# Four GNN layers on one core: the last layer by seven products of half matrices, logits spread on TensorE, statistics stored in two parts

## The chip, the cores and the metric

The kernel runs on one core of one Trainium2 chip. The metric is the device time of one execution in microseconds (us); the median of 12 runs of the kernel before is 2025.46 us (2020.86 to 2029.03). The engines of the core are TensorE (PE in the profile; PEld is its weight load), VectorE (DVE), ScalarE (ACT), GpSimd (POOL) and SyncE (SP). Each takes its instructions in the order in which they were compiled. SP, ACT and POOL also issue DMAs, each on its own queue; SPq, ACTq and POOLq in the profile are these issues.

## The reference

Input are x, 2708 nodes by 256 features, and adj, a sparse 2708 x 2708 matrix with a full diagonal, all float32. Four layers follow each other, each as `x = layernorm(x + layer(x, adj))`:

- layer 0: `adj @ (x * W)`
- layer 1: attention with four heads of 64 features over the mask `adj > 0`, then a layer norm
- layer 2: two supports and two GRU cells. With A = adj without its diagonal: `edge_output = gru(A @ h, h)`, and for each of three heads `hW = h @ W`, a logit e per node from the sums of hW over its neighbours, `att = softmax` over the columns with A > 0 of e, and `att * A @ hW`. The mean over the heads goes through the second GRU cell, `node_output`. The result is `diag * (edge_output + node_output)`
- layer 3: `h = adj @ (x @ neigh_W.T) / (rowsum(adj) + 1)` and `z = [x, h] @ lin_W.T`

The logits e depend on the column alone, so that the softmax needs for each row and head a maximum and a denominator: the row statistics.

## The kernel before, in words

The nodes lie in 22 tiles of 128 rows (NT; the last has 20). Six spans of 4 or 3 tiles order the work of layer 1 and the edge half of layer 2. For the node half the matrix is cut in two halves of 1354 nodes (NH, 11 tiles: MH), and the columns of both halves in three units of 512, 512 and 330 (`units`).

Layer 2, edge half: `edge_logits` (L484) makes the logits of each span, writes them to DRAM (`e_d`, L507, six stores on POOL's queue), and three DMAs on ACT's queue (L788) read them back as `e_b`, the same 2708 numbers on all 128 partitions, per head. `row_stats` then makes the statistics of each row tile: a custom VectorE operation (L816) for the maximum and an exponential with a sum on ACT (L821), 66 of each. `edge_sums` (L241) multiplies A by h for a span, `edge` runs the first GRU cell on it (`gru_t`, L724) and stores the result (`edge_d`, L830). `xt_d` and `edge_d` are DRAM tensors with x and the edge output transposed. At the end `store_rows` turns the statistics of all tiles (`store_stats`, L757-773: transposes on PE, a copy to `sr` on ACT, stores on POOL's queue). The node half reads them back on SP (`load_stats`, L882).

Layer 2, node half (L1062-1126): for each unit, each head and each of 11 pairs of row tiles (c and c + 11) a step loads the blocks of adj (`load_blocks`, L898 on SP, 9 or 7 DMAs of two 128 x 128 blocks each; a block on the diagonal is masked on POOL, L901), builds four quarter blocks of attention (ACT Relu L1076, Exp L1079, DVE L1080), forms three sums of quarters on DVE (L1085-1088), and runs seven products instead of eight (L1099) into seven PSUM banks, with sums of the quarters of x that `x_sums` makes on POOL, four subtractions of 128 x 128 for each c. The seven accumulators are `m1`, `m26`, `m75`, `m43`. After 11 steps they are added up to `y`.

What follows from a unit is cut into tasks, run in the one PSUM bank left, after the third and the sixth product of a step (`between`): `project` (L928) multiplies by the head's weights, `node` loads `xt2` and `et` (L234 on SP), runs the second GRU cell (`cell`, L945, L959) and the row ends: `node_rows` (L983), `rows_turned` (L997), `rows_end` (L1006). The last makes the input of layer 3, `h3` (x @ neigh_W.T and lin_W already multiplied in), and the part of the output that doesn't need adj, stored as `y3_d` (L1013). The tasks of the last unit, four of `project` and 37 of `node`, run after the last product, with eight PSUM banks (L1127-1130).

Layer 3 (`layer3`, L1133-1146) loads for each row tile a strip of adj, 128 rows of 11 KB in one DMA on SP (L180), and multiplies it by the 22 tiles of h3, each in two passes of 256 columns (`strip_matmul`, L201). The last operations of a tile: load `o` from y3_d (L1139 on SP), one DVE operation (L1142), layer norm (L148-159, with a power on POOL, L153), the store of the output on POOL's queue (L1146).

The instructions of an engine are put in order at compile time by a list scheduler. A DMA issued on SP or ACT waits for the DMA eight before it, since eight semaphores are shared in turn.

Of the kernel before, what the change touches and what calls it, by code (L numbers as in the profile page):

```python
# [27 lines left out]
def kernel(  # L28
# [100 lines left out]
    e_d = dram.tile([K, N], F32, name="e_d")  # L129
# [3 lines left out]
    xt_d = dram.tile([P, FC, N], F32, name="xt_d")  # L133
    edge_d = dram.tile([P, FC, N], F32, name="edge_d")
# [96 lines left out]
    def load_columns(pool, d, lo, w, tag, bufs=1):  # L231

        dst = pool.tile([P, FC, W], F32, tag=tag, name=tag, bufs=bufs)
        nc.sync.dma_start(dst[:, :, :w], d[:, :, lo : lo + w])  # L234
        return dst
# [3 lines left out]
    edges = []  # L239

# [60 lines left out]
    if True:  # L301
# [14 lines left out]
        if True:  # L316
# [145 lines left out]
            if True:  # L462
# [21 lines left out]
                def edge_logits(pool, rows):  # L484

                    evs = rows.tile([P, len(banks), W], F32, tag="supt", name="evs", bufs=2)
                    for b, w, acc in zip(banks, bw, pu):
                        full = len(b) * CT
                        parts = pool.tile([P, W], F32, tag="parts", name="parts")
                        nc.scalar.copy(parts[:full, :w], acc[:full, :w])  # L490
                        pe = ps_t.tile([P, 4, P], F32, tag="tr", name="pe").rearrange("p i q -> p (i q)")
                        nc.tensor.matmul(
                            pe[: K * TILES, :w], add_parts[:full].rearrange("p k j -> p (k j)"), parts[:full, :w],
                            start=True, stop=True,
                        )
                        ev = evs[: K * TILES, b.start // TILES]
                        nc.scalar.copy(ev[:, :w], pe[: K * TILES, :w])
                        nc.vector.scalar_tensor_tensor(ev[:, :w], ev[:, :w], ALPHA, ev[:, :w], ALU.mult, ALU.max)
                        pc = ps_t.tile([P, 4, P], F32, tag="tr", name="pc")
                        for i in range(w // P):  # L500
                            nc.tensor.transpose(
                                pc[:, i, : K * TILES], ev[:, i * P : (i + 1) * P], ident[: K * TILES, : K * TILES]
                            )
                        for j, g in enumerate(b):
                            lo, hi = spans[g]
                            gw = width(lo, hi)
                            nc.gpsimd.dma_start(e_d[:, lo * P : lo * P + gw], ev[j : K * TILES : TILES, :gw])  # L507
                            nc.vector.tensor_scalar(
                                e_neg[:, lo:hi, :],
                                pc[:, : hi - lo, : K * TILES].rearrange("p i (k j) -> p i k j", j=TILES)[:, :, :, j],  # L510
                                -1.0, None, ALU.mult,
                            )
# [37 lines left out]
                def layer1_logits(pool, t, m, fill, split, gap):  # L550
# [3 lines left out]
                    nc.gpsimd.dma_start(xt_d[:, :, t * P : t * P + n], xt[:, :, :n])  # L554
# [202 lines left out]
    def store_stats(ps, pool, lo, hi):  # L757

        at, w = lo * P, width(lo, hi)
        pt = ps.tile([P, 4, P], F32, tag="tr", name="pst")  # L760
# [5 lines left out]
        sr = pool.tile([2 * K, W], F32, tag="sr", name="sr")  # L766
# [11 lines left out]
    with pool("e_work") as ework:  # L778
        with (
# [7 lines left out]
            for k in range(K):  # L787
                nc.scalar.dma_start(e_b[:, k], bcast(e_d[k], N))  # L788
# [8 lines left out]
            def row_stats(i):  # L797
# [15 lines left out]
                for k in range(K):  # L813
                    z = rows.tile([P, N], F32, tag="z", name="z", bufs=3)
# [11 lines left out]
            def edge(g, supt, xt):  # L826
                at, w = spans[g][0] * P, width(*spans[g])
                yt = ework.tile([P, FC, W], F32, tag="yt", name="yt")
                gru_t(ps_g, ework, yt, supt, xt, w, wih, whh, b_edge)
                nc.scalar.dma_start(edge_d[:, :, at : at + w], yt[:, :, :w])  # L830

            stored = 0

            def store_rows(done):

                nonlocal stored
                while stored < done:
                    n = 1
                    while n < 4 and stored + n < done and order[stored + n] == order[stored] + n:
                        n += 1  # L840
                    store_stats(ps_e, rows, order[stored], order[stored] + n)
                    stored += n

            for g, (lo, hi) in enumerate(spans):
                for i in range(lo, hi):
                    row_stats(i)
                last = g + 1 == len(spans)
                if last:
                    store_rows(lo)
# [7 lines left out]
            store_rows(NT)  # L857
# [5 lines left out]
    with (  # L863
# [20 lines left out]

        def load_blocks(u, c):
# [21 lines left out]
        ts = []  # L907

        def x_sums(c):
            tt = nleft.tile([P, 4, P], F32, name=f"xq{c}")  # L910
            b11, b12 = xs[c][:, :P], xs[c][:, P:]
            b21, b22 = xs[c + MH][:, :P], xs[c + MH][:, P:]
            nc.gpsimd.tensor_tensor(tt[:, 0], b12, b11, ALU.subtract)
            nc.gpsimd.tensor_tensor(tt[:, 1], b22, tt[:, 0], ALU.subtract)
            nc.gpsimd.tensor_tensor(tt[:, 2], b12, b22, ALU.subtract)
            nc.gpsimd.tensor_tensor(tt[:, 3], b21, tt[:, 1], ALU.subtract)
            ts.append(tt)
# [63 lines left out]
        shared = {}  # L981
# [32 lines left out]

        def node(u, est):
# [3 lines left out]
            for h in range(2):  # L1019
                lo = h * NH + a  # L1020
                xt, et = nxt or [load_columns(nleft, d, lo, w, tag) for d, tag in ((xt_d, "xt2"), (edge_d, "et"))]
# [3 lines left out]
                tiles, at = [], 0  # L1025
                for t, c0, c1 in pieces(lo, w):
                    src = yt[:, :, at : at + c1 - c0]
                    at += c1 - c0
                    if c1 - c0 < sz(t):
                        first = t not in shared  # L1030
                        if first:
                            shared[t] = nleft.tile([P, FC, P], F32, name=f"yt{t}")
                        nc.gpsimd.tensor_copy(shared[t][:, :, c0:c1], src)
                        if first:
                            continue
                        src = shared[t]
                    tiles.append((t, src))
                got, turned = [], []
                for i in range(len(tiles) + 2):
# [9 lines left out]
                    if i == 1 and h == 0:  # L1049
                        nxt = [load_columns(nleft, d, NH + a, w, tag) for d, tag in ((xt_d, "xt2"), (edge_d, "et"))]  # L1050
# [11 lines left out]
        for u, (_, w) in enumerate(units):  # L1062
            est = [nleft.tile([P, FC, W], F32, tag="est", name="est", bufs=3) for h in range(2)]
            for k in range(K):
                m1 = ps_a.tile([P, W], F32, tag="m1", name="m1")
                m26, m75, m43 = (ps_a.tile([P, 2, W], F32, tag=nm, name=nm) for nm in ("m26", "m75", "m43"))
                for c in range(MH):
                    if u == 0 and k == 0:
                        x_sums(c)
                    blk = load_blocks(u, c)  # L1070
                    pa = []
                    for i in range(2):
# [8 lines left out]
                        pa += [p[:, 0, :w], p[:, 1, :w]]  # L1081
                    a11, a21, a12, a22 = pa
                    s = nright.tile([P, 3, W], F32, tag="s", name="s", bufs=2)
                    s1, s2, s4 = (s[:, i, :w] for i in range(3))
                    nc.vector.tensor_tensor(s1, a21, a22, ALU.add)  # L1085
                    nc.vector.tensor_tensor(a21, a21, a11, ALU.subtract)  # L1086
                    nc.vector.tensor_tensor(s2, s1, a11, ALU.subtract)
                    nc.vector.tensor_tensor(s4, a12, s2, ALU.subtract)
                    tt = ts[c]
                    for i, (dst, lt, rt) in enumerate((  # L1090
                        (m1, xs[c][:, :P], a11),
                        (m26[:, 0], xs[c + MH][:, :P], a12),
                        (m75[:, 0], tt[:, 2], a21),
                        (m75[:, 1], tt[:, 0], s1),
                        (m26[:, 1], tt[:, 1], s2),
                        (m43[:, 0], tt[:, 3], a22),
                        (m43[:, 1], xs[c + MH][:, P:], s4),
                    )):
                        nc.tensor.matmul(dst[:, :w], lt, rt, start=(c == 0), stop=(c == MH - 1))  # L1099
                        if i in (2, 5):  # L1100
                            between()
                    if u == 0 and k == 0 and c == 2:
                        node_w = load_weights()
                    if c == MH - 3:
# [5 lines left out]
                t1 = nleft.tile([P, W], F32, tag="m1s", name="m1s")  # L1110
                nc.scalar.copy(t1[:, :w], m1[:, :w])

                y = nleft.tile([P, FC, 2, W], F32, tag="yk", name="yk")
                yq = y.rearrange("p f h w -> p (f h) w")[:, :, :w]
                nc.vector.tensor_tensor(
                    yq[:, 0::3], t1[:, None, :w].to_broadcast([P, 2, w]), m26[:, :, :w], ALU.add
                )
                nc.vector.tensor_tensor(
                    yq[:, 1:3], yq[:, 3:4].to_broadcast([P, 2, w]), m75[:, :, :w], ALU.add
                )  # L1120
                nc.vector.tensor_tensor(yq[:, 3], yq[:, 1], m75[:, 1, :w], ALU.add)
                nc.vector.tensor_tensor(yq[:, 1:3], yq[:, 1:3], m43[:, :, :w], ALU.add)
# [3 lines left out]
            later.append(node(u, est))  # L1126
        ps_stack.close()  # L1127
# [19 lines left out]

    layer3()

# [246 lines left out]
```

## Time and profile before

| | |
|---|---|
| median of 12 runs | 2025.46 us |
| the profiled execution | 2024.36 us |
| its span | 2022.6 us |
| mean granted clock of TensorE | 0.981 |
| busy: PE, DVE, ACT, POOL | 95%, 67%, 43%, 16% |
| passes of layer 3 on PE (968) | 209.25 us |
| loads of adj for layer 3 on SP | 22 of up to 1408 KB |
| loads of blocks for the node half on SP (L898) | 825 issues, 0.54 to 1.76 us each, median 0.61 |
| landing after issue: 54 and 74 KB blocks, o, out | 2.5, 2.0, 3.5 us |

The span is what the engines' instructions cover; the execution's own time is 1.8 us longer. A line of a chain or a timeline gives the start in us from the span's start, the length in us, the engine, the line of the kernel and the number of instructions in a row. A line of waits gives the engine and line that waited, after the arrow what ended the wait, then the sum in us, how many times, and the longest. A line of windows gives a stretch, and for each engine its busy time and the number of its instructions.

### The profile page before, as it was taken

What the parts mean: (1) busy time and instruction counts of PE and PEld (TensorE: products, weight loads), DVE (VectorE), ACT (ScalarE), POOL (GpSimd) and SP (SyncE); (2) the same over time, 40 slices, a digit from 0 to 9 for tenths busy, and PEclk for the clock granted to TensorE, in tenths of its full rate; (3) what the DMA queues carried; (4) which work ended last, traced back from release to release, by engine and by line L of the source; (5) the groups of instructions that cost most, each with busy time, mean ns of one, the idle gap of its engine ahead of it and who ended that gap; (6) DMA issues with size and microseconds to landing.
All of it is one profiled execution on the core that took longest, in us unless ns stands there. A gap on an engine that the chain in (4) does not pass through costs nothing. (4 is left out here: it accounts for less than half of the span.)

```text
span 2022.6 us, 21703 instructions
## 1 busy us (share of the span) xinstructions
PE 1916.6 (95%) x7454; PEld 1032.2 (51%) x7454; DVE 1358.0 (67%) x2123; ACT 871.9 (43%) x995; POOL 329.8 (16%) x532
## 2 busy tenths in 40 slices
PE   8999999999999899999679999999999999889997
PEld 7888722222333334455333444444445656458886
DVE  4334388898897489999478789685876868431111
ACT  0100145446413167777656766565565656110000
POOL 0212110015324220111221001010100111011111
PEclk9999999999999999999889999999999999889999
DMA  8344333432104786664357766454553535214543
GB/s 283 130 149 164 107 132 116 143 132 96 34 9 111 269 262 213 201 210 139 109 157 200 193 175 175 123 161 111 158 151 99 151 94 133 81 43 175 188 178 107
DMA packets 334115, 296.49 MB, mean 147 GB/s; under 512 B 85836, under 2 KB 311030, under 8 KB 322946
## 3 DMA queue, kind: packets, MB, share of 16 engines
q1 hardware_dynamic: 318474, 245.28, 39.9%
q0 software_dynamic: 8512, 41.14, 5.6%
q10 hardware_dynamic: 7008, 8.58, 1.2%
q8 instruction: 61, 1.00, 0.2%
q14 instruction: 60, 0.49, 0.1%
HBM read 283.16 MB, written 11.76 MB: 146 GB/s over the span
## 5 line engine op out<-in xcount | busy, mean ns | idle before, releaser
L201 PE MATMUL acc<-turn,strip 128*128 128x256 f32 (+1 forms) x1804 | 396.4, 379 | 0.0
L201 PEld LDWEIGHTS acc<-turn,strip 128*128 128x128 f32 (+1 forms) x1804 | 331.7, 186 | 53.4 <-issue 1.3
L654 DVE SCALAR_TENSOR_TENSOR p<-fall_b,rise,mask 128x1024 f32<-128x1024 f32 (+1 forms) x264 | 298.9, 1154 | 37.4 <-PE den L645 19.8
L1076 ACT ACTIVATE p<-st,e_neg 128x1024 f32<-128x1024 f32 (+1 forms) x198 | 206.8, 1046 | 222.9 <-PE m L1099 218.4
L636 PE MATMUL acc<-p,h 128*64 128x512 f32 (+2 forms) x1056 | 228.0, 560 | 4.7 <-DVE p L654 2.7
L1080 DVE TENSOR_TENSOR p<-p,blk 128x1024 f32<-128x1024 f32 (+1 forms) x132 | 147.4, 1121 | 101.9 <-ACT p L1079 57.4
L816 DVE CUSTOM_DVE_ANT_0 z<-e_b,none 128x2708 f32<-128x2708 f32 (+1 forms) x66 | 196.5, 2983 | 15.2 <-DMA e_b<-e_d 15.2
L821 ACT ACTIVATE z<-z,st 128x2708 f32<-128x2708 f32 (+1 forms) x66 | 168.5, 2554 | 65.0 <-DVE st L816 63.5
L1099 PE MATMUL m<-p,x 128*128 128x512 f32 (+1 forms) x396 | 170.1, 548 | 25.7 <-DVE p L1080 22.2
L1079 ACT ACTIVATE p<-p 128x1024 f32<-128x1024 f32 (+1 forms) x198 | 188.9, 956 | 5.6
L1099 PE MATMUL m<-p,xq 128*128 128x512 f32 (+1 forms) x396 | 182.8, 544 | 1.6 <-DVE p L1086 0.9
L254 PE MATMUL s<-blk,x 128*128 128x512 f32 (+2 forms) x416 | 165.4, 552 | 4.7 <-DMA blk<-in_adj_t_dram 3.5
L1099 PE MATMUL m<-s,xq 128*128 128x512 f32 (+1 forms) x396 | 168.2, 542 | 0.0
L153 POOL TENSOR_TENSOR bn_rs<-bn_rs,neg_half 128x1 f32<-128x1 f32 (+1 forms) x110 | 75.5, 688 | 425.6 <-DVE bn_rs L152 425.5
L636 PEld LDWEIGHTS acc<-p,h 128*64 128x64 f32 x1056 | 65.2, 137 | 150.5 <-issue 119.1
L645 PE MATMUL den<-p,h 128*32 128x512 f32 (+2 forms) x1056 | 125.0, 554 | 2.3 <-DVE p L654 1.9
L1099 PEld LDWEIGHTS m<-p,x 128*128 128x128 f32 x396 | 74.8, 191 | 101.5 <-issue 62.2
L254 PEld LDWEIGHTS s<-blk,x 128*128 128x128 f32 x416 | 78.7, 192 | 82.1 <-issue 67.4
L1142 DVE SCALAR_TENSOR_TENSOR o<-acc,rdeg,o 128x256 f32<-128x256 f32 (+1 forms) x22 | 10.6, 483 | 155.8 <-PE acc L201 155.8
L1099 PEld LDWEIGHTS m<-p,xq 128*128 128x128 f32 x396 | 74.6, 190 | 78.1 <-issue 56.6
L1099 PEld LDWEIGHTS m<-s,xq 128*128 128x128 f32 x396 | 74.2, 190 | 74.5 <-issue 64.8
L167 ACT COPY xt<-tr 128x256 f32<-128x256 f32 (+1 forms) x44 | 16.0, 364 | 209.2 <-PE tr L165 203.4
(200 smaller groups left out, 2366.5 us busy)
## 6 DMA issues: line engine op xcount, KB each, us to landing
strip<-in_adj_t_dram SPq DMA_DIRECT2D x41, 1408.0 KB, 6.0
blk<-in_adj_t_dram SPq DMA_DIRECT2D x411, 128.0 KB, 2.7
turn<-in_adj_dram SPq DMA_DIRECT2D x22, 1354.0 KB, 5.8
turn<-in_adj_t_dram SPq DMA_DIRECT2D x204, 128.0 KB, 2.7
blk<-in_adj_t_dram SPq DMA_DIRECT2D x84, 256.0 KB, 5.7
arow<-in_adj_dram POOLq DMA_DIRECT2D x10, 1354.0 KB, 6.8
turn<-in_adj_dram POOLq DMA_DIRECT2D x10, 1354.0 KB, 6.7
st<-st SPq DMA_DIRECT2D x12, 512.0 KB, 4.5
```

The lines of the kernel that those rows point to most:

```text
L153: nc.gpsimd.tensor_tensor(rstd[:n], rstd[:n], neg_half[:n], ALU.pow)
L201: nc.tensor.matmul(acc, s[:, c, :n], rhs(c), start=(c == 0), stop=(c == NT - 1))
L254: nc.tensor.matmul(acc[f][:, :w], xs[c][:, f * P : (f + 1) * P], s[:, c - c0, :w], start=(c == 0), stop=(c == NT - 1),)
L636: nc.tensor.matmul(acc[s][i * HD : (i + 1) * HD, :ws], hs[c][:, 2 * q + i, :HD], ps[i][:, p0 : p0 + ws], **flags,)
L645: nc.tensor.matmul(den[j : j + CT, :ws], hs[c][:, 2 * q + i, HD + 1 - CT :], ps[i][:, p0 : p0 + ws], **flags,)
L654: nc.vector.scalar_tensor_tensor(p[:, :w], falls[g // 2][:, 2 * q + i, :w], rise[:, c, 2 * q + i : 2 * q + i + 1], mask[:, c, at : at + w] ...
L816: nc.vector.tensor_tensor_reduce(out=z[:n], in0=e_b[:n, k, :], in1=none[:n], scale=-1.0, scalar=HIGHEST, op0=ALU.add, op1=ALU.min, accum_o ...
L821: nc.scalar.activation(z[:n], z[:n], AF.Exp, scale=-1.0, bias=st[:n, t, 0, k : k + 1], accum_out=den[:n])
L1076: nc.scalar.activation(p[:, :, :w], st_k[:, :, :w], AF.Relu, scale=-1.0, bias=e_neg[:, at, k : k + 1])
L1079: nc.scalar.activation(p[:, :, :w], p[:, :, :w], AF.Exp, scale=-1.0)
L1080: nc.vector.tensor_tensor(p[:, :, :w], p[:, :, :w], blk[:, i, :, :w], ALU.mult)
L1099: nc.tensor.matmul(dst[:, :w], lt, rt, start=(c == 0), stop=(c == MH - 1))
```

## The change

1. Layer 3 is done by the same seven products as the node half, three units of 11 steps, 7 products a step. The blocks of adj go straight from DRAM into the tiles of the quarter blocks, one DMA per block of at most 128 x 128 and per row tile: 18, 18 and 14 in a step (`load_pairs`). Sums of the quarters of h3 are made on DVE (`quarter_sums`), `step` and `sums` are the node half's code made into functions. The row ends of layer 3 are tasks (`rows3`): per tile two transposes back, then as before, but `o` is loaded on POOL's queue, into three buffers that it shares with `y`. Tiles cut by a unit's edge are put together by copies on POOL (`by_tiles`).
2. The steps of layer 3's first unit whose h3 tiles are ready before the last unit of layer 2 ends, seven of eleven, run while the last 41 tasks of layer 2 are done, a task after each of the seven products. What is left of the tasks runs before the eighth step.
3. `e_b` is made by TensorE: a product with a column of the identity spread over 128 columns, once per span and head (18), then copied from PSUM, half by ACT and half by DVE. `e_d` is gone. `z` has two buffers in place of three.
4. The statistics of the first unit's rows (9 tiles) are stored as soon as the spans with them are done; the other four runs of tiles are tasks of the node half (`other_stats`).
5. `x_sums` on POOL becomes `quarter_sums` on DVE. `xt_d` and `edge_d` are one tensor per span, and the node's loads of `xt2` and `et` are issued on POOL's queue, in pieces by span.

```diff
-                nc.scalar.dma_start(e_b[:, k], bcast(e_d[k], N))
+                for g, (lo, hi) in enumerate(spans):
+                    at, w = lo * P, width(lo, hi)
+                    ev, j = e_rows[g]
+                    r = k * TILES + j
+                    pb = ps_g.tile([P, W], F32, tag="gate", name="pb")
+                    nc.tensor.matmul(
+                        pb[:, :w], ident[:, r : r + 1].to_broadcast([P, P]), ev[:, :w], start=True, stop=True
+                    )
+                    if g % 2:
+                        nc.vector.tensor_copy(e_b[:, k, at : at + w], pb[:, :w])
+                    else:
+                        nc.scalar.copy(e_b[:, k, at : at + w], pb[:, :w])
...
-                    z = rows.tile([P, N], F32, tag="z", name="z", bufs=3)
+                    z = rows.tile([P, N], F32, tag="z", name="z", bufs=2)
...
-                    store_rows(lo)
...
-            store_rows(NT)
+                if lo >= first and not stored:
+                    stored = first
+                    for run in runs(order[:first]):
+                        store_stats(
+                            ps_e.tile([P, W], F32, tag="pst", name="pst"),
+                            rows.tile([2 * K, W], F32, tag="sr", name="sr", bufs=2), *run,
+                        )
...
+        def load_pairs(u, c, dst):
+            a, w = units[u]
+            for h in range(2):
+                at = 0
+                for t, lo, hi in pieces(h * NH + a, w):
+                    for i in range(2):
+                        nc.sync.dma_start(dst[i][:, h, at : at + hi - lo], adj_t[t, :, c + i * MH, lo:hi])
+                    at += hi - lo
...
-        def x_sums(c):
-            tt = nleft.tile([P, 4, P], F32, name=f"xq{c}")
-            b11, b12 = xs[c][:, :P], xs[c][:, P:]
-            b21, b22 = xs[c + MH][:, :P], xs[c + MH][:, P:]
-            nc.gpsimd.tensor_tensor(tt[:, 0], b12, b11, ALU.subtract)
...
+        def quarter_sums(b, c):
+            tt = nleft.tile([P, 4, P], F32, tag=f"xq{c}", name=f"xq{c}")
+            b11, b12 = b[c][:, :P], b[c][:, P:]
+            b21, b22 = b[c + MH][:, :P], b[c + MH][:, P:]
+            nc.vector.tensor_tensor(tt[:, 0], b12, b11, ALU.subtract)
...
+        def other_stats():
+            for run in runs(order[first:]):
+                store_stats(bank(), nleft.tile([P, W], F32, tag="m1s", name="sr")[: 2 * K], *run)
+                yield
...
+        def rows3(u, y):
+            a, w = units[u]
+            for h in range(2):
+                for t, src in by_tiles(h * NH + a, w, lambda at, n: y[:, :, h, at : at + n], shared3):
+                    n = sz(t)
+                    o = nleft.tile([P, F], F32, tag="y", name="o", bufs=3)
+                    nc.gpsimd.dma_start(o[:n], y3_d[t])
+                    pt = bank()
+                    for f in range(FC):
+                        nc.tensor.transpose(pt[:n, f * P : (f + 1) * P], src[:, f, :n], ident)
+                    nc.vector.scalar_tensor_tensor(
+                        o[:n], pt[:n, :F], rdeg[:n, t : t + 1], o[:n], ALU.mult, ALU.add
+                    )
+                    layernorm(o, o, n)
+                    nc.gpsimd.dma_start(out[t * P : t * P + n, :], o[:n])
+                    yield
+
+        lead = sorted(range(MH), key=lambda c: max(ends_at[c], ends_at[c + MH]))
+        hq = {}
+        for u, (_, w) in enumerate(units):
+            m = accumulators()
+            for i, c in enumerate(lead):
+                early3 = u == 0 and max(ends_at[c], ends_at[c + MH]) + 1 < len(units)
+                if u == 0:
+                    if not early3:
+                        while urgent or later:
+                            between()
+                    hq[c] = quarter_sums(h3, c)
+                pa = [nright.tile([P, 2, W], F32, tag=f"p{j}", name=f"p{j}", bufs=3) for j in range(2)]
+                load_pairs(u, c, pa)
+                step(m, pa, h3, hq[c], c, w, i == 0, i == MH - 1, range(7) if early3 else (2, 5))
+            later.append(rows3(u, sums(m, w)))
...
-    layer3()
```

## The prediction, made before the result was known

> **What bounds the kernel now.** I read the page first (busy time, the chain by line), then the chain in order of time around the start and end of layer 3, then windows of busy time, the waits in the two stretches where TensorE stands, and last the issue times on SP, the queue on which the change puts the most new work.
>
> ```profile
> PE 1916.6 (95%) x7454; PEld 1032.2 (51%) x7454; DVE 1358.0 (67%) x2123; ACT 871.9 (43%) x995; POOL 329.8 (16%) x532
> ```
>
> TensorE is the bound over the whole span; whatever takes its passes away can gain, if nothing else takes its place. The chain in order of time gives the last products of layer 2, its row ends, and layer 3 (columns: start, length, what):
>
> ```profile
> 1701.99 26.65 PE m L1099 x96
> 1732.97 6.37 PE bank L934 x16
> 1739.33 13.33 PE bank L959 x48
> ...
> 1801.04 1.89 PE bank L1010 x4
> 1802.93 209.25 PE acc L201 x968
> ```
>
> The products of layer 2 end at 1728.6. The row ends of the last unit take until 1802.9, and layer 3 is 968 passes of 256 columns without a hole, 0.216 us each, or 0.844 ns a column. Busy time in four stretches (columns: stretch, its length, busy PE, PEld, DVE, ACT, POOL, then clock, DMA share, GB/s):
>
> ```profile
> 720.00:976.00 256.00, 248.93 (x647) 122.83 (x645) 255.09 (x309) 191.11 (x172) 39.33 (x34) 0.99 0.60 191
> 1003.00:1024.00 21.00, 1.27 (x2) 0.50 (x2) 4.54 (x2) 11.54 (x12) 20.91 (x49) 0.50 0.53 178
> 1730.00:1803.00 73.00, 56.36 (x169) 32.13 (x170) 30.10 (x72) 15.00 (x34) 7.75 (x15) 0.86 0.18 63
> 1803.00:2012.00 209.00, 209.00 (x968) 179.66 (x968) 35.28 (x106) 0.33 (x1) 24.11 (x43) 1.00 0.46 164
> ```
>
> From 720 to 976 VectorE and TensorE are both full. From 1003 to 1024 only POOL works. The tail of layer 2 leaves TensorE about 17 us idle; layer 3 leaves VectorE and SP nearly free. The waits around the start of layer 2 and of the row statistics (us in total, times, longest):
>
> ```profile
> DVE p L1080 <- POOL blk L901: 24.0, 2, 23.3
> PE m L1099 <- DVE p L1080: 22.2, 1, 22.2
> ```
>
> ```profile
> DVE z L816 <- DMA e_b<-e_d: 15.2, 3, 9.0
> DVE dtmp L807 <- DMA turn<-in_adj_dram: 6.2, 1, 6.2
> ```
>
> SP's issues, back to back (start, length, what, count):
>
> ```profile
> 15.97 1.45 SPq L410 DMA_DIRECT2D strip<-in_adj_t_dram  x3
> ...
> 48.30 0.33 SPq L448 DMA_DIRECT2D gamma_b<-in_L_gnn_gamma_dram  x1
> 48.67 0.43 SPq L449 DMA_DIRECT2D beta_b<-in_L_gnn_beta_dram  x1
> ...
> 1253.06 5.79 SPq L898 DMA_DIRECT2D turn<-in_adj_t_dram  x9
> ```
>
> A lone issue of a plain load (128 rows, one run each) holds SP 0.33 us; one that follows at once 0.43, with 0.04 between, so 0.474 a piece (three at L410: 1.45). The two-block loads of L898 cost 5.79 / 9 = 0.64 to 0.655 a piece, rows of 216 bytes as much as rows of 512: the bytes don't set it.
>
> **A: the logits by products.** Gone: the 15.2 us wait for e_b; the 6.2 us wait for the adjacency row beside it should shrink, since the three 1354 KB broadcasts fill the DMA engines there. Added on TensorE: 2708 columns x 3 heads x 2 passes x 0.844 ns = 13.7 us; on VectorE 9 copies at 0.4 to 0.69 (a 512-column operation) = 5.3; on ACT 9 at about 0.57, into idle time (191 of 256). VectorE would thus gain 21.4 - 5.3 = 16 us. But TensorE idles only 16.6 us between 690 and 996 (4.7, 7.1 and 4.8 in three windows), and 13.7 of it is now used: it can gain 2.9 at most, and loses 13.7 if none of the products fits a hole. z in two buffers for three costs nothing while VectorE (2.98 us a row and head) is slower than ACT's exponential (2.55). I take +2, between -3 and +14, nearer the first since the holes lie just where the products run.
>
> **B: statistics in two parts, half-matrix sums of x off POOL.** Now the first diagonal mask (L901) waits on POOL behind 44 subtractions of 0.41 us, so TensorE restarts at 1024.6. The changed kernel has the 44 on VectorE behind the last edge-GRU operation (995.4) and ahead of the first product: 44 x 0.21 to 0.29 (L810, the same shape) = 10 to 12 us, then 1.2 for the product: 1007.5. The remaining stores of statistics leave the path, because the units' first statistics are stored a span earlier. Gain 17; 25 if the subtractions overlap the GRU's end; 5 if block loads still queue behind the last edge stores. I take -17. The two transposes of statistics ahead of the first product cost under 1 us each (L763), and the rest runs between products.
>
> **C: layer 3.** TensorE: 154 products of 512 columns (four passes took 1.72, so 0.86 a product) and 77 of 330 (1.11, so 0.555) are 132 + 43 = 175 us for 209. But the strips came in 22 loads, and the blocks come in 18, 18 and 14 loads a step of the three units: 550 on SP, all 128 rows with one run of at most 512 bytes.
>
> *Early part*, seven steps between the row ends: turnover of the accumulators 3, products 7 x 6.0 = 42, row ends 52 (the window's 56.4 busy above, 48 by passes), and one bank in place of eight: each of the 41 tasks waits for the copy of the one before, mostly covered by the 0.86 us product between them; 0.2 each, 8 us. Together 105 us; 92 if nothing stalls, 125 if every task shows its copy (0.57 + 0.1). SP's 18 loads (8.5 us) hide in a step of 15.
>
> *After it*, SP cannot have run further ahead than the three buffers of p0 and p1 allow: two steps are loaded, the third is freed by the last early step. It has 36 + 198 + 154 = 388 loads to issue, and at 0.474 that is 184 us; then 2.5 to land (54 to 74 KB loads of L898) and 2.6 for VectorE's four half-matrix sums and the last product. TensorE's own need is smaller: 24 + 66 + 43, transposes 8, two turnovers of 3.5: 148. So SP ends last, at 8.5 us a step against 6.0. Layer 3 ends 105 + 184 + 5 = 294 after the last product of layer 2, where it now ends 283.6 after it: **+10.4**. The price of an issue has no row of exactly this kind. Lowest: 0.33 + 0.04 = 0.372 (lone issues). Highest: 0.655 (two blocks). I take 0.474, the row of the same form; every 0.01 is 3.9 us. VectorE (2.8 us a step, and 0.25 x 44) stays hidden under SP's 8.5.
>
> The Trainium skill speaks to this price twice, on its page DMA: Bandwidth & Descriptors. Under Anatomy of one DMA it puts a sequencer's dispatch at about 50 ns; by that SP would be free and the total about 1999. Under Bandwidth it asks for 1 MiB per transfer and gives 0.95 us for 64 KB; an estimate with 388 of these one after another would be about 2223. This trace agrees with neither: L898's 128 KB loads hold SP 0.6 us each, and go out every 0.655 us though each lands 2.6 us after its issue, so four overlap.
>
> **D: the end.** Now 0.17 us of TensorE are left after 2012.0; one short tile follows:
>
> ```profile
> 2012.20 0.47 DVE L1142 SCALAR_TENSOR_TENSOR o<-acc,rdeg,o 20x256 f32<-20x256 f32 x1 [7.10 <-PE acc L201]
> ...
> 2014.94 0.54 POOL L1146 DMA_DIRECT2D out_dram<-o  x1 [0.73 <-DVE o L159]
> ```
>
> That is 10.4 us to the end of the span, 7.7 of them behind the last store's issue. Afterwards the last unit's sums come first (four operations of 0.5 to 0.84: 2.6 us past the last product), and then seven tiles in three buffers, whose loads and stores share POOL's queue. First round: store issues at 5.3, 7.1 and 7.7. Each next load waits for a store to land (3.5) and lands itself in 2.3, then VectorE and POOL need 2.2: stores at 13.3, 15.6, 16.2. The seventh tile: load at 16.8, store at 21.3, then the same 7.7: 29. **+18.6**; +10 with landings of 2 us, +25 if POOL's 0.7 us powers queue up.
>
> POOL also takes the node's loads over from SP, some 16 issues of 0.55 us; behind them wait L901's masks, powers and row stores. POOL is busy 16%, so I cost it at nothing; a 5 us delay of a mask in each of three units would be 15.
>
> **Sum**, against the profiled execution's 2024.4 (its span 2022.6 and 1.8 around it; 1.1 below the median): +2 - 17 + 10.4 + 18.6 = +14, so 2038.4, and 2039 against the median. With the issue price p: 1854.5 + 388 p; it breaks even at p = 0.438.
>
> **Rivals.** (1) *Faster:* SP issues a 512-byte-row load at the lone price. For it: 0.33 is what most plain loads show; against it: those had SP to themselves, and each of the three that followed at once took 0.43 or more. At 0.372 SP needs 144 + 5 and TensorE 148: 1999. It decides below 0.438. (2) SP pays L898's 0.655, because the source's rows are as far apart: 2109. Against it: L410's pieces have that row distance too. (3) The early part stalls: one bank, and a VectorE queue that also carries sums; 0.7 a task: 2058. (4) The hole at 1003 stays, as block loads or masks wait for something else, POOL's node loads among them: 2055.
>
> **How the numbers follow.** Forecast 0.52, own range 2024 to 2053 (price 0.45 to 0.50, early part ±6); (1) 0.20; (2) 0.08; (3) 0.12; (4) 0.08. The range 2000 to 2062 leaves out (2) and the lower half of (1), and holds the rest. 0.2% or 4 us is what a measurement tells from no change. Of the forecast 0.40 is slower, 0.09 within, 0.03 faster; (1) is faster throughout, 0.19 and 0.01 within; (2), (3), (4) are slower: 0.68, 0.10, 0.22.
>
> **What would show it.** SP's line of the new loads: x550, median near 0.43, and in units 1 and 2 waits of TensorE or VectorE for DMA p0 or p1, PE near 70% busy there. The hole: TensorE back at about 1007. No wait for e_b, the edge GRU's end unmoved. Behind the last product some 29 us. Wrong if SP's issues fall under 0.43 back to back, if PE is over 95% busy in units 1 and 2, or if the early part is far from 105 us.

## The result, and the profile after

The changed kernel takes 2037.55 us (median of 13 runs), the kernel before 2024.97 us (52 runs): a ratio of 1.0066, with a 95% interval of 1.0057 to 1.0075, that is 13 us slower. The forecast was 2039 us, and slower. The profiled execution of the changed kernel took 2034.18 us, its span is 2032.3 us, 9.7 us longer than that of before.

Where these 9.7 us come from is seen by cutting both spans at the same events (starts of TensorE's passes, us from the span's start). Each column is one profile. In the twelve profiles of the changed kernel and its variants, which are alike up to there, the last pass of the edge GRU lies between 991.1 and 997.7, so the first row tells nothing.

| | before | after | stretch before | stretch after | difference |
|---|---|---|---|---|---|
| last pass of the edge GRU | 992.4 | 991.7 | | | -0.7 |
| first product of the node half | 1022.7 | 1004.9 | 30.3 | 13.2 | -17.1 |
| last product of layer 2 | 1729.3 | 1716.9 | 706.6 | 712.0 | +5.4 |
| last product of layer 3 | 2011.8 | 1996.4 | 282.5 | 279.5 | -3.0 |
| end of the span | 2022.6 | 2032.3 | 10.8 | 35.9 | +25.1 |

TensorE is less busy than before (1916.6), and VectorE has 105 us more to do:

```profile
PE 1908.8 (94%) x7028; PEld 948.9 (47%) x7028; DVE 1462.6 (72%) x2364; ACT 878.9 (43%) x1007; POOL 352.5 (17%) x529
```

Windows of the changed kernel (stretch, length, busy PE, PEld, DVE, ACT, POOL, clock, DMA share, GB/s): the logits and statistics, the former hole, then layer 3 while the row ends run, after them, and in its later units.

```profile
720.00:976.00 256.00, 253.01 (x663) 124.69 (x662) 243.48 (x301) 185.97 (x171) 45.90 (x40) 0.99 0.62 195
...
1003.00:1024.00 21.00, 18.47 (x39) 7.81 (x40) 19.59 (x27) 15.80 (x16) 5.29 (x8) 0.88 0.90 269
...
1717.00:1822.00 105.00, 102.10 (x293) 49.68 (x292) 57.72 (x125) 15.44 (x34) 12.54 (x21) 1.00 0.42 119
1822.00:1840.00 18.00, 18.00 (x44) 7.83 (x43) 11.81 (x19) 0.68 (x2) 1.93 (x4) 1.00 0.49 135
1840.00:1915.00 75.00, 63.39 (x147) 26.04 (x145) 32.75 (x69) 0.59 (x1) 12.22 (x21) 0.98 0.52 145
1915.00:1996.00 81.00, 60.28 (x179) 35.45 (x179) 39.22 (x92) 0.44 (x1) 14.84 (x26) 0.89 0.46 121
```

The hole at 1003 is gone (1.3 us of TensorE there before, 18.5 now). The path to the first product of the node half goes over POOL now, not over VectorE alone (the first line is of the chain, the second of the timeline):

```profile
997.29 6.08 POOL blk L936
```

```profile
1003.39 2.82 DVE L1175 TENSOR_TENSOR p<-p,blk 128x1024 f32<-128x1024 f32 x2 [0.34 <-POOL blk L936]
```

VectorE does 41 of the 44 subtractions from 994.7 to 1003.0. Beside them a single diagonal mask on POOL takes 6.08 us, where the masks of `blk` have a median of 0.47, and VectorE then waits 0.34 us for it.

From 720 to 976 the bound has passed from VectorE (255.1, now 243.5) to TensorE (248.9, now 253.0). TensorE is full in layer 3 while tasks are left, and stands 12 and 21 us in the later units. What it waits for there (us in total, times, longest):

```profile
DVE s L966 <- DMA p<-in_adj_t_dram: 57.7, 12, 6.7
...
PE m L979 <- DVE p L967: 13.4, 15, 2.7
PE m L979 <- DMA p<-in_adj_t_dram: 13.1, 8, 2.9
```

VectorE and TensorE both wait for blocks. The issue line of these blocks (duration ns, least, median and most) and their landing:

```profile
L917 SPq DMA_DIRECT2D p<-in_adj_t_dram x550: 327/430/1635, 1707.3 to 1991.2; - x184
...
DMA to landing us min/median/max: 1.7/1.9/4.1
```

Each lands 1.9 us after its issue, but 550 of them take SP from 1707.3 to 1991.7. In a step that waits for nothing, 18 issues take 8.44 us, so that one follows the other every 0.471 us ((8.44 - 0.43) / 17).

The end of the changed kernel, in order of time (in brackets the idle time before, and what ended it):

```profile
2003.48 0.59 POOL L1209 DMA_DIRECT2D out_dram<-o  x1 [0.75 <-DVE bn_mv L148]
...
2006.52 0.54 POOL L1201 DMA_DIRECT2D o<-y  x1
2007.74 1.11 POOL L1201 DMA_DIRECT2D o<-y  x2 [0.68 <-DMA out_dram<-o]
2009.02 0.48 DVE L1205 SCALAR_TENSOR_TENSOR o<-bank,rdeg,o 128x256 f32<-128x256 f32 x1 [3.41 <-DMA o<-y]
...
2015.36 0.53 POOL L1201 DMA_DIRECT2D o<-y  x1
2017.49 0.47 DVE L1205 SCALAR_TENSOR_TENSOR o<-bank,rdeg,o 20x256 f32<-20x256 f32 x1 [3.02 <-DMA o<-y]
...
2020.23 0.56 POOL L1209 DMA_DIRECT2D out_dram<-o  x1 [0.73 <-DVE o L157]
```

Three rounds of load, row end and store, as forecast: VectorE waits 3.41 and 3.02 us for a load of o. What the loads wait for is only in part a store: the ones at 2007.74 wait 0.68 us for it to land, while those at 2006.52 and 2015.36 follow POOL's instruction before them at once.

### The profile page after: what moved, and what is told of

Its sections match the earlier page's. It is cut to its first block, busy times and chain, and to the rows that moved or that the text cites. A ratio compares the mean times of both kernels' runs of the same rounds, so it can differ in the third digit from the quotient of the medians.

```text
span 2032.3 us, 21956 instructions
## 1 busy us (share of the span) xinstructions
PE 1908.8 (94%) x7028; PEld 948.9 (47%) x7028; DVE 1462.6 (72%) x2364; ACT 878.9 (43%) x1007; POOL 352.5 (17%) x529
## 4 chain that ended last, share of the span: by engine, by line
PE 68%; DVE 13%; DMA 5%; SPq 5%; issue 4%; POOL 3%; ACT 1%; DVEq 0%; ACTq 0%; POOLq 0%
PE m L979 26%; PE acc L199 9%; PE acc L643 9%; PE bank L1040 5%; PE den L652 5%; DVE z L843 4%; PE s L258 4%; PE bank L1015 3%; SPq L917 3%; PE gate L744 2%; SPq L933 2%; PE bank L1091 2%; DVE p L661 1%; POOL bn_rs L151 1%; PE acc L416 1%
## 5 line engine op out<-in xcount | busy, mean ns | idle before, releaser
L979 PE MATMUL m<-p,xq 128*128 128x512 f32 (+1 forms) x528 | 249.0, 556 | 30.1 <-DVE p L967 16.8
L979 PE MATMUL m<-s,xq 128*128 128x512 f32 (+1 forms) x528 | 230.1, 552 | 0.0
L199 PE MATMUL acc<-turn,strip 128*128 128x256 f32 (+1 forms) x836 | 187.1, 379 | 0.0
L979 PE MATMUL m<-p,x 128*128 128x512 f32 (+1 forms) x396 | 171.1, 551 | 12.2 <-DVE p L1175 8.3
L199 PEld LDWEIGHTS acc<-turn,strip 128*128 128x128 f32 (+1 forms) x836 | 151.9, 185 | 23.5 <-issue 0.2
L979 PEld LDWEIGHTS m<-p,xq 128*128 128x128 f32 x528 | 98.1, 193 | 136.8 <-issue 75.2
L966 DVE TENSOR_TENSOR s<-p,p 128x512 f32<-128x512 f32 (+1 forms) x132 | 83.6, 634 | 89.3 <-DMA p<-in_adj_t_dram 65.2
L979 PEld LDWEIGHTS m<-s,xq 128*128 128x128 f32 x528 | 101.2, 195 | 97.0 <-issue 80.9
```

Of the source, the lines that this page charges most:

```text
L199: nc.tensor.matmul(acc, s[:, c, :n], rhs(c), start=(c == 0), stop=(c == NT - 1))
L979: nc.tensor.matmul(dst[:, :w], lt, rt, start=start, stop=stop)
```

## The experiments

All are edits of the changed kernel unless said otherwise. Ratios are to the kernel before, with 95% intervals.

**What paces layer 3.**

```diff
-  nc.sync.dma_start(dst[i][:, h, at : at + hi - lo], adj_t[t, :, c + i * MH, lo:hi])
+  (nc.sync, nc.scalar)[i].dma_start(dst[i][:, h, at : at + hi - lo], adj_t[t, :, c + i * MH, lo:hi])
```

> The changed kernel, but of layer 3's block loads those for the second half of the row tiles (p1) are issued on ACT's queue instead of SP's. Theory (the number of issues on SP paces layer 3 at 0.471 us each): each queue then needs 9 x 0.471 = 4.2 us a step, less than TensorE's 6.0 (3.9 in the last unit, against 3.3), TensorE becomes the bound again, layer 3 ends about 235 us after layer 2's last product instead of 279.6, and the whole takes about 1992 us. Rival (the loads are paced by what the two queues share, the descriptor generation or the DMA engines, or by 1.9 us of landing): the pitch on each queue doubles or the landings grow, and the time stays near 2037.

2011.2 us, ratio 0.9938 (0.9922 to 0.9955): 26 us less than the change. The two issue lines:

```profile
L917 SPq DMA_DIRECT2D p<-in_adj_t_dram x275: 327/430/2320, 1713.1 to 1964.1; - x138
L917 ACTq DMA_DIRECT2D p<-in_adj_t_dram x275: 334/442/1647, 1714.8 to 1965.3; - x138
```

The price of an issue stays as it was on SP, and ACT pays 0.44 beside it, so the queue was the bound, not what the queues share. The landing grew from 1.9 to 2.4 us (medians), and the layer became shorter all the same. Steps of the second unit go at 6.0 us. Layer 3 still takes 249.5 us and not 235: the row ends last until 115 us after layer 2's last product instead of 104, since ACT's copies for them stand in order behind loads that wait for a buffer. The Trainium skill (Trainium Kernel Development and Optimization, Key Constraints) says that issuing DMAs from several engines only saves the sequencer's issue time; here that time was what was lacking.

```diff
-  nc.sync.dma_start(dst[i][:, h, at : at + hi - lo], adj_t[t, :, c + i * MH, lo:hi])
+  for q in range(0, P, P // (2 if u == 1 else 1)):
+      e = q + P // (2 if u == 1 else 1)
+      nc.sync.dma_start(
+          dst[i][q:e, h, at : at + hi - lo], adj_t[t, q:e, c + i * MH, lo:hi]
+      )
```

> The changed kernel, but in layer 3's second unit every block is loaded by two DMAs of 64 rows in place of one of 128: 36 issues a step for 18, the same bytes and rows. Theory (SP's time is a price per issue, 0.471 us, whatever a DMA moves): 198 more issues are 93 us more, about 2130, and the median issue stays at 0.43 us. Rival 1 (the price is one per row moved): half the rows cost half, 2037. Rival 2 (the price is 0.33 us of issue and the rest follows the rows): between, about 2090.

2196.8 us, ratio 1.0836 (1.0805 to 1.0868): worse than any theory. The issues of 64 rows have a median of 0.595 us and follow each other every 0.64, those of 128 rows in the other units of the same run every 0.47. So 396 x 0.64 in place of 198 x 0.47 is 160 us, which is what the run lost. SP's price is neither one per byte nor one per row; a DMA of half the rows costs more than a whole one. Why is not shown. The window of that unit:

```profile
1843.00:2075.00 232.00, 95.88 (x152) 34.02 (x152) 36.90 (x74) 0.59 (x1) 11.79 (x21) 0.69 0.20 53
```

The DMA engines are busy 20% here and TensorE works 41% of the time: both wait for SP.

**What beginning early is worth.**

```diff
-  early3 = u == 0 and max(ends_at[c], ends_at[c + MH]) + 1 < len(units)
+  early3 = False
```

> The changed kernel, but layer 3 begins after all 41 tasks of layer 2 are done, in place of running seven steps between them. Theory (the early steps hide 41 tasks of 47 us and, more, SP's issues: 30 steps of loads then lie behind the tasks, 496 x 0.471 = 234 us): layer 3 ends about 320 us after layer 2's last product instead of 279.6: about 2078. Rival (beginning early saves only what TensorE idled in the tail of the kernel before, 17 us): 2054.

2038.0 us, ratio 1.0064 (1.0045 to 1.0083): the same as the change. The starts of layer 3's first eleven steps agree with the change's to 0.1 us. The scheduler had moved the steps between the tasks by itself, as only the data order them, so the edit undid nothing, and the run told nothing of the question. The order of the steps was turned round instead:

```diff
-  lead = sorted(range(MH), key=lambda c: max(ends_at[c], ends_at[c + MH]))
+  lead = sorted(range(MH), key=lambda c: -max(ends_at[c], ends_at[c + MH]))
```

> The changed kernel, but layer 3's first unit takes its steps in the reverse order: the four steps whose h3 tiles are ready last come first. (With the tasks written ahead of the steps but the old order of steps, the scheduler put the instructions in the same order as in the change, so that run told nothing on this.) No product of layer 3 can then run before the last row ends. Theory (the early steps hide the 41 tasks of 47 us, and with them SP's issues, of which 30 steps, 496 x 0.471 = 234 us, now lie behind the tasks): the tasks take about 75 us, layer 3 ends about 320 us after layer 2's last product instead of 279.6: about 2077. Rival (beginning early saves only the 17 us that TensorE idled in the tail of the kernel before): 2054.

2107.8 us, ratio 1.0394 (1.0375 to 1.0414): layer 3 ends 347.5 us after layer 2's last product instead of 279.5. Now the tasks have no products between them, and one bank:

```profile
1722.00:1823.00 101.00, 69.07 (x174) 32.64 (x173) 36.43 (x85) 13.89 (x30) 9.60 (x17) 0.83 0.13 37
```

It is 101 us up to the second step, and 110 to the last row end, and not the 75 that I put in. That the one bank is the reason is argued, since no run gave these tasks more banks. From that step's start to the last product it is 247 us, for 234 of issues and the landing. Beginning early is worth 68 us to this layer, twice what the seven products save in passes (209 to some 175 us); in this order of steps the kernel is 4% slower than the one before.

**Layer 3 undone, and the logits alone.** In the first, the strips of the kernel before are back, after the tasks, with their `o` loads; the second is the kernel before with the 18 products and copies for `e_b`, and `z` in two buffers.

```diff
-  for u, (_, w) in enumerate(units):
-      m = accumulators()
...
-      later.append(rows3(u, sums(m, w)))
+  layer3()
```

> The changed kernel with layer 3 as before (strips, passes of 256 columns, after the last unit's tasks): parts A and B alone. Theory (the hole at 1003 closes by 19.7 us, of which 6 to 8 come back as holes in the first steps of the node half; A is about 0): 2025 - 12 = about 2013. Rival 1 (the 8 us lost inside layer 2 belong to what the seven products of layer 3 bring along): 2005. Rival 2 (A costs what B gains): 2025.

2017.9 us, ratio 0.9962 (0.9951 to 0.9972), 7.6 less than before. The node half takes 713.4 us in it, about as long as in the change: the 5 us lost there don't come from layer 3.

```diff
-  nc.scalar.dma_start(e_b[:, k], bcast(e_d[k], N))
+  for g, (lo, hi) in enumerate(spans):
...
+      nc.tensor.matmul(pb[:, :w], ident[:, r : r + 1].to_broadcast([P, P]), ev[:, :w], start=True, stop=True)
+      if g % 2:
+          nc.vector.tensor_copy(e_b[:, k, at : at + w], pb[:, :w])
+      else:
+          nc.scalar.copy(e_b[:, k, at : at + w], pb[:, :w])
...
-  z = rows.tile([P, N], F32, tag="z", name="z", bufs=3)
+  z = rows.tile([P, N], F32, tag="z", name="z", bufs=2)
```

> The kernel before with part A alone: logits spread by 18 products, z in two buffers. Theory (A is worth about nothing, because TensorE's and VectorE's holes between 690 and 996 are used up by its own products and copies): between 2022 and 2028, most likely 2025. Rival (the wait of 15.2 us for e_b was a true loss on the path of VectorE): 2012. Rival (the products lie on TensorE's path): 2038.

2024.1 us, ratio 0.9995 (0.9981 to 1.0009): no change. The windows show why:

```profile
690.00:720.00 30.00, 29.49 (x74) 13.54 (x73) 27.48 (x35) 21.35 (x23) 1.64 (x2) 1.00 0.68 220
720.00:976.00 256.00, 253.99 (x661) 125.97 (x660) 242.38 (x299) 184.58 (x169) 41.91 (x34) 0.99 0.61 189
```

VectorE's wait is gone, but TensorE is full in both stretches.

**The end.**

```diff
-  y = nleft.tile([P, F], F32, tag="y", name="y", bufs=3)
+  y = nleft.tile([P, F], F32, tag="y", name="y", bufs=6)
...
-  o = nleft.tile([P, F], F32, tag="y", name="o", bufs=3)
-  nc.gpsimd.dma_start(o[:n], y3_d[t])
+  o = nleft.tile([P, F], F32, tag="y", name="o", bufs=6)
+  nc.scalar.dma_start(o[:n], y3_d[t])
```

> The changed kernel with six buffers for y and o in place of three, and the loads of o in layer 3 on ACT's queue. Theory (the end is paced by o's three buffers, whose loads wait for stores of 2.9 us landing, and by POOL's queue): six of the last seven tiles have their o before the last product, the last store is issued about 16 us after the last product instead of 23.5, and the time falls by about 8, to 2029. If the drain of GpSimd at the end (5.9 us, 2.2 before the change) comes from the number of DMAs on its queue, some 4 us more: 2025. Rival (the end is paced by the power on POOL and the layer norm): no change, 2037.

2035.6 us, ratio 1.0059 (1.0042 to 1.0076), only 2 less than the change. The end behind the last product fell from 35.9 to 26.5 us, the last store is issued 16.6 us after it, and the drain fell. But layer 3 took 287.6 us instead of 279.5: SP pauses up to 2.8 us after some of ACT's loads, until a load of o has landed, 8.6 us in all (the change has no such wait):

```profile
SPq L917 <- DMA o<-y: 8.6, 7, 2.8
```

The loads of both queues share the eight semaphores, and layer 3 has no spare issue time on SP. With the loads left on POOL:

```diff
-  y = nleft.tile([P, F], F32, tag="y", name="y", bufs=3)
+  y = nleft.tile([P, F], F32, tag="y", name="y", bufs=6)
...
-  o = nleft.tile([P, F], F32, tag="y", name="o", bufs=3)
+  o = nleft.tile([P, F], F32, tag="y", name="o", bufs=6)
```

> The changed kernel with six buffers for y and o in place of three, the loads of o on POOL's queue as in the change. Theory (the loads of o at the end wait for stores to land; on ACT's queue the same loads cost SP 6 us by their place among the eight shared semaphores): the layer's end stays at 280 us after layer 2's last product, and the end behind it falls from 36 to about 29 us: 2031. Rival (loads issued on POOL early delay its row ends in layer 3, or the end is paced by POOL's own operations): 2037.

2026.5 us, ratio 1.0006 (0.9991 to 1.002): 11 us less than the change. The end is 30.0 us, layer 3 278.5; that is 7 of the 11, and the node half was 3 shorter (709.2; see the node half below). The last store is issued 17.9 us after the last product instead of 23.8.

**The 5 us of the node half.** Its first steps in the changed kernel (SP's issues, then pieces of the chain):

```profile
1008.64 13.85 SPq L933 DMA_DIRECT2D blk<-in_adj_t_dram  x18
1022.58 5.79 SPq L933 DMA_DIRECT2D turn<-in_adj_t_dram  x9
1028.48 11.68 SPq L933 DMA_DIRECT2D blk<-in_adj_t_dram  x18
1040.25 5.79 SPq L933 DMA_DIRECT2D turn<-in_adj_t_dram  x9
```

```profile
1033.00 0.61 SPq L933
1033.66 2.58 DMA blk<-in_adj_t_dram
1036.55 1.23 DVE p L1175
```

SP issues without a pause, 5.85 us a step against 6.0 of products, and the chain runs over it. Two runs tried to put SP ahead: the blocks of the second half of the columns on ACT's queue in the first three steps,

```diff
-  nc.sync.dma_start(s[:, :, h, at : at + hi - lo], adj_t[t, :, c : NT : MH, lo:hi])
+  (nc.scalar if h and loaded <= 3 else nc.sync).dma_start(s[:, :, h, at : at + hi - lo], adj_t[t, :, c : NT : MH, lo:hi])
```

> The changed kernel, but in the first three steps of the node half the blocks of the second half of the columns are loaded on ACT's queue, so that SP reaches the fourth step some 8 us earlier. Theory (the changed kernel starts the node half 18 us earlier with SP behind: 9 loads of 0.655 us a step against 6.0 us of products, so the holes of 6 to 8 us at 1013, 1063 and 1077 are waits for blocks): the holes shrink and the time falls by 4 to 8 us, to about 2031. Rival (the holes come from the statistics' tasks or from POOL, which now carries the node's loads): 2037 as before.

and the six loads of the node's weights on ACT's queue.

```diff
-  wih, whh = weights(nleft, "wih", n_wih), weights(nleft, "whh", n_whh)
+  wih, whh = weights(nleft, "wih", n_wih, nc.scalar), weights(nleft, "whh", n_whh, nc.scalar)
...
-  lwn = load_lwn(nleft)
+  lwn = load_lwn(nleft, nc.scalar)
...
-  nc.sync.dma_start(wk[:, k], gat_w[k].rearrange("(c p) j -> p c j", p=P))
+  nc.scalar.dma_start(wk[:, k], gat_w[k].rearrange("(c p) j -> p c j", p=P))
```

> The changed kernel, but the node half's weights (six loads, 3.4 us of SP at 1005, between the blocks of its second and third step) are issued on ACT's queue. In the run with the first blocks on ACT's queue these six loads still stood in SP's order and waited longer, so SP did not get ahead. Theory (SP issues without a pause from 1008.6 to 1090, so each us of other issues ahead of that is a us of TensorE's waiting): the third step's blocks come 3.4 us earlier, the holes of 7 us in the first 80 us of the node half shrink by about 3, and the time falls to about 2034. Rival (the holes belong to something else, as the statistics' tasks): 2037.

2037.2 us (ratio 1.0063, 1.0044 to 1.0082) and 2040.1 us (1.0059, 1.0042 to 1.0077): no gain. In the first, SP reached the blocks of its fourth step no sooner (1014.0), because seven of its loads went out only from 1000.2 on and the weights' loads behind them took 8 us. In the second, TensorE stood 11.9 us in the node half instead of 12.2, and the first product came 15.9 us after the edge GRU instead of 13.2; ACT has the loads ahead of its exponentials there. That SP's issues make these holes is what the chain shows; it was not shown by taking them away.

Nor is all of the 5.4 us SP's. Cut by heads, the change loses 2.0 us in the first head, 1.9 in the second and 2.0 in the first head of the third unit, and gains 0.5 in the rest. In the second head TensorE worked at half its clock for 4 us (last section), which costs some 2 us. The third piece is a hole of 1.8 us while VectorE waits for a store of `y` to land, as `y` has three buffers:

```profile
1579.54 0.48 DVE L1072 SCALAR_TENSOR_TENSOR y<-bank,diag,x 128x256 f32<-128x256 f32 x1 [2.00 <-DMA y<-y]
```

All four runs with six buffers lack it: this head takes 78.6 or 78.7 us in them, as before (78.6), and 80.6 to 82.7 in the others with the change's node half. Why the same three buffers cost nothing before the change was not tested.

**Together.** The p1 loads go to ACT's queue from the eighth step on alone, with six buffers:

```diff
-  def load_pairs(u, c, dst):
+  def load_pairs(u, c, dst, split):
...
-  nc.sync.dma_start(dst[i][:, h, at : at + hi - lo], adj_t[t, :, c + i * MH, lo:hi])
+  (nc.scalar if i and split else nc.sync).dma_start(dst[i][:, h, at : at + hi - lo], adj_t[t, :, c + i * MH, lo:hi])
...
-  o = nleft.tile([P, F], F32, tag="y", name="o", bufs=3)
+  o = nleft.tile([P, F], F32, tag="y", name="o", bufs=6)
...
-  load_pairs(u, c, pa)
+  load_pairs(u, c, pa, not early3)
```

> Six buffers for y and o, and the loads of p1 on ACT's queue only from layer 3's eighth step on, so that no load stands ahead of ACT's copies for the tasks. Theory (with all steps split, the time was 2011 and the tasks ended 16 us later than in the change, because ACT's copies stood behind loads that waited for a buffer): the early part takes 105 us again, the rest is bound by TensorE at 6.0 and 3.9 us a step: layer 3 ends about 235 us after layer 2's last product, the end behind it is 29 us, the time about 1989. Rival (the early part was not held by ACT): 2004, the six buffers alone.

1982.8 us, ratio 0.9802 (0.9764 to 0.9839): faster than both kernels. Layer 3 takes 239.6 us, the row ends are done after 104.1, and the end takes 28.4. TensorE in layer 3's second and third unit:

```profile
1835.00:1906.00 71.00, 68.67 (x170) 31.16 (x169) 41.42 (x84) 0.58 (x1) 13.13 (x23) 0.98 0.64 174
1906.00:1952.00 46.00, 42.09 (x158) 27.69 (x157) 28.48 (x79) 0.43 (x1) 14.72 (x26) 1.00 0.63 167
```

97% and 91%, where the change had 85% and 74%. A last run adds the weights on ACT's queue and the last unit's output stores on SP's:

```diff
-  nc.gpsimd.dma_start(out[t * P : t * P + n, :], o[:n])
+  (nc.sync if u == 2 else nc.gpsimd).dma_start(out[t * P : t * P + n, :], o[:n])
```

> Six buffers, the loads of p1 on ACT's queue from layer 3's eighth step on, the node's weights on ACT's queue, and the output stores of layer 3's last unit on SP's queue, which has nothing left to load by then. Theory (POOL's queue paces the last seven tiles with 0.57 us of issue and 0.56 us of power each, and its stores take 2.9 us to land): the end behind the last product falls from 28.4 to about 23 us, the weights give 3: about 1976. Rival (neither is on the path): 1983.

1985.3 us, ratio 0.9781 (0.9753 to 0.981): not told apart from the one before. The end fell to 25.6 us, half of the way to the 23 expected, but the first product came 15.2 us after the edge GRU instead of 13.1.

## Why the prediction was right, and where its terms were not

Direction and size came out: 2039 forecast, 2037.55 measured. The mechanism was right in its main lines, a hole that closes, SP's issues as the pace of layer 3, and a long end. That the sum is within 2 us is luck, since its terms are off by more and cancel.

- **A, the logits**: +2 forecast, -0.7 between the two profiles, which is less than two profiles tell apart, and nothing in the run of this part alone. Right, for the reason given: TensorE's holes are used up.
- **B, the statistics and the sums of x**: -17 forecast to the first product, -17.1 measured, with both ends some 2 us off: before the change TensorE starts again at 1022.7, not 1024.6, and after it at 1004.9, not 1007.5, since 41 subtractions ahead of the product took 8.3 us on VectorE (0.20 each) and not 10 to 12. What ended last was not VectorE but a mask on POOL, which took 6.08 us beside the subtractions. Nor did only POOL work from 1003 to 1024 before the change: ACT was busy 11.5 of the 21 us. What the step missed, and put at nothing, is what comes next: SP has 5.85 us of issues in a step of 6.0, and the hole had let it load ahead. Started 18 us earlier, the node half gives back 5.4 us, some 4 of them on a chain over SP and in the half clock after it, 2 waiting for a store of `y`. I had asked whether POOL's new loads would delay masks: one of them, 0.5 us, stands ahead of the first mask on the chain, and none on the chain over the holes that follow.
- **C, the price of an issue**: 0.474 forecast from L410 and L448/L449, 0.471 measured, and nothing of rival (1) at 0.372 or (2) at 0.655. The two figures that it weighs from the Trainium skill (DMA: Bandwidth & Descriptors, Anatomy of one DMA and Bandwidth) stand there for DMAs issued on GpSimd; an issue on SP took 0.43 us here. Its cause was right, as the run with two queues shows: SP, not the landings, paces the layer.
- **C, the early part**: 105 us for seven steps was the mis-sized term. After 105 us TensorE had done the 41 tasks and 8.8 steps. The turnover took 0.7 us and not 3, the tasks 47.5 and not 52, and the single bank cost nothing with a product between the tasks; the run with no products between them (101 us up to its second step) suggests that the 8 us were put on the wrong case. SP had 345 loads left and not 388. So layer 3 came to 279.5 instead of 294: -3 in place of +10.4.
- **D, the end**: +18.6 forecast, +25.1 measured. The three rounds came, the first store 1.8 us later (7.1 behind the start of the last product), the others with it, the last at 23.8 instead of 21.3. Inside a round one price was wrong and another made up for it: a store landed in 2.0 to 2.4 us, not 3.5 (nor the 2.9 of later expectations), but POOL's queue, where loads, powers and stores follow each other, took the time instead. The 7.7 us behind the last store were taken over from before, but were 12.1: GpSimd's drain grew (below). With six buffers the rounds are gone and 6 us with them.
- **What would show it**: the waits, the hole and the count of issues showed as written. TensorE's 70% in units 1 and 2 were 85% and 74%.

The errors of A (-2.7), of C (-13.4), of D (+6.5) and of the node half (+5.4) cancelled to within 5 us of the sum.

## What to carry to other kernels

Count a change's DMAs by the issuing queue and price them by an issue that follows another of the same form, not by a lone one: 0.43 + 0.04 us here against 0.33; a product that is cheaper by a sixth brought 3 us to layer 3, since it came with 25 times as many issues on one queue, and 43 us once two queues shared them and `y` and `o` had six buffers. Where a bubble closes, ask what was loading ahead in it. And what is added behind the last product is paid in full, here 25 us and the largest loss of the change, so the last tiles need their own buffers.

## What the runs showed of the hardware that was not expected

- An issue of 64 rows held SP 0.595 us where one of 128 rows held it 0.430, in the same run.
- GpSimd's last two instructions before the end, the reset of its DMA semaphores and a drain, took 0.69 + 2.11 us with 125 DMAs issued on its queue (logits alone), 0.71 + 2.19 with 131 (before), 1.19 + 4.15 with 143 (old layer 3, and o on ACT's queue), 1.49 + 5.38 with 158 (the last run) and 1.63 + 5.95 with 165 (after). 4.7 us of the change's loss are this.
- A mask of 128 x 128 on POOL took 6.08 us beside VectorE's subtractions, and one of 74 columns 6.48 us at 1086.7, where VectorE also worked without a pause; the medians are 0.47 (`blk`) and 0.62 (`turn`). That VectorE holds POOL up fits both, but no run separates the two.
- After a hole of 3.9 us on TensorE, from 1077.6 to 1081.5 in the changed kernel, the granted clock was 0.50 up to 1085.5, and the passes of 512 columns took 0.86 us instead of 0.43. In the kernel before, a hole of 3.4 us at 1093.5 left it at 1.00:

```profile
1070.00:1077.00 7.00, 7.00 (x17) 3.04 (x16) 6.35 (x8) 5.88 (x6) 0.94 (x2) 1.00 0.65 176
1081.50:1085.50 4.00, 3.99 (x5) 1.85 (x6) 4.00 (x6) 0.00 (x0) 0.56 (x1) 0.50 0.66 184
```
